# Two channels to a block matrix: the banded convolutions of layers 2 and 3 in four array tiles instead of sixteen

## The chip, the cores and the metric

The kernel runs on one core of one Trainium2 chip. A core has TensorE (PE, matrix products), VectorE (DVE), ScalarE (ACT), GpSimd (POOL), SyncE (SP, which here only issues transfers), and 16 DMA engines that all queues share. The metric is the device time of one launch in microseconds. Everything is fp32.

## The reference

Four layers with residuals act on x of 8 images, 384 channels, 32x32 pixels; each takes a group norm of its input first.

```python
x = x + L0(gn(x))   # 3 depthwise 3x3 convs + 1x1 convs give q, k, v; attention, 8 heads; 1x1; batch norm
x = x + L1(gn(x))   # 4 experts (384 -> 384 -> 384, relu), 2 of them weighted for each pixel
x = x + L2(gn(x))   # depthwise 7x7 convolution, reflected edges, bias
x = x + L3(gn(x))   # below

def L3(x):
    # three branches, k = 1, 3, 5; the channels are split into 4 chunks of 96:
    # chunks 0 and 2 go through a small MLP (96 -> 12 -> 96), chunks 1 and 3 through a depthwise kxk conv
    x1, x2, x3 = branch(x, 1), branch(x, 3), branch(x, 5)
    a = (x1 + x2 + x3).mean((2, 3))
    g = gelu(a @ fusion_w1 + b1) @ fusion_w2 + b2
    w = softmax(g.reshape(8, 384, 3) over the three branches)
    comb = x1 * w[0] + x2 * w[1] + x3 * w[2]
    return einsum("bchw,cd->bdhw", comb, proj_w) + proj_b
```

## The kernel before

Channels lie on partitions, in three tiles of 128 (`ct` 0 to 2); NC is 3, B 8, N 1024 pixels, W and H 32, P 128, HB 4.

Depthwise convolutions are made on TensorE. An image row of 32 pixels lies along partitions (VectorE transposes 32x32 blocks, L985), four channels to a column of 128 partitions. A horizontal convolution of one channel with one row k of its kernel is then a banded 32x32 matrix; the K rows are accumulated in PSUM, each reading the image shifted by one row. TensorE's array is split into 16 tiles of 32x32: partition group i (32 rows of the array) and column group j take the channel that belongs to (i, j, c). So a chunk c of 16 channels is K x 16 matmuls of 256 columns (8 images x 32) or, for unit 1 of layer 3 with half the images a tile, 128 columns. In the trace one fp32 matmul is two instructions: 224 for a chunk with K = 7, 160 for K = 5, 96 for K = 3.

Layer 2 (L1282 on) runs ct over three tiles and c over 8 chunks. Two chunks fill a PSUM group `ps` of four banks, then ScalarE copies it (`evict`, L1236) to `o`; there are two such groups. The weights `w` of a chunk (edges of the reflection folded in by two GpSimd adds, L1052) come by `next_weights` (L1046), three buffers, issued on SP's queue after the chunk that frees one. SP takes its transfers in order, and waits where one of them waits. When all of ct is done, `finish_all` works on its images: `finish` (L1152 on) transposes back on VectorE (L1157), adds bias and residual `r2` (L1159; loaded by SP at L1154 from `r2mem`), takes statistics for the next norm, and stores y to DRAM (L1162). These steps are interleaved with the matmuls of the next ct. During ct 1 `prepare` reads xn of the third channel tile from `x2mem` (L1143) and transposes it for ct 2, in the same VectorE queue.

After the seventh chunk of ct 2 the norm of layer 3 starts for the first two channel tiles (`norm01`): small matmuls (L167), VectorE, GpSimd (L135), then `prepare3` loads y again, ScalarE normalizes it (L200) and VectorE transposes it (L1218). Then comes unit 1 (`convolve3`, L1260), which holds channels of one half tile of the convolved chunks for both halves of the batch, with `finish` of ct 2 and the norm of the third tile beside it, then unit 0, the first whole tile, with the MLPs (L1449) in between, fusion and softmax of the branch weights, and at last the projection (L1653 on, from 3314 us). `reorder` copies y from DRAM to DRAM into the order of the transposed channels, for the 1x1 branch and the residual. `pair(q)` and `begin` fetch and weigh the convolved chunks for the projection.

Channel orders: ORDER_B is the plain order of layer 3's chunks; ORDER_A has partitions and chunks swapped, so that (i, j, c) of a transposed tile comes out in ORDER_B. Layer 1 writes its result `r` in ORDER_A to `r2mem` (`pass_on`, L1000) with the rows permuted, four transfers for each channel tile of an image. The order of instructions on every engine is the program's in these stages.

Of the kernel before, what the change touches and what calls it, by code (L numbers as in the profile page):

```python
# [1 line left out]

# [34 lines left out]

CHUNKS = (1, 3, 0, 2)
ORDER_B = np.concatenate([np.arange(96) + 96 * c for c in CHUNKS])
ORDER_A = ORDER_B.reshape(NC, 4, 4, 8).swapaxes(1, 2).ravel()  # L40
# [32 lines left out]
def conv_mixer_kernel(ctx: ExitStack, tc: tile.TileContext, a: dict, out: bass.AP):  # L73
# [18 lines left out]
    def group_matrix(order, pool, gp, gps):  # L92
# [11 lines left out]
        if order == "A":  # L104
            gta = gp.tile([C // GS, C], FP, name="gta")
            for ct in range(NC):
                cols = slice(ct * P, (ct + 1) * P)
                nc.gpsimd.tensor_copy(
                    gta[:, cols].rearrange("g (i j c) -> g i j c", i=4, j=4),
                    gt[:, cols].rearrange("g (j i c) -> g i j c", i=4, j=4),  # L110
                )
            gt = gta
# [883 lines left out]
    def pass_on(r, b):  # L996

        for ct in range(NC):
            for i in range(4):
                nc.sync.dma_start(  # L1000
                    out=r2mem[ct][:, b, :].rearrange("(j i c) n -> i j c n", i=4, j=4)[i],
                    in_=r[32 * i : 32 * i + 32, ct, :],
                )
# [9 lines left out]
    for b, h in EARLY:  # L1013
# [11 lines left out]

    lw = lwpool.enter_context(
        tc.tile_pool(name="lw", bufs=3, side="right", reuse_waits="tile")
    )
    weights = {}
    ahead = iter(  # L1030
        [(K7, ct, c) for ct in range(NC) for c in range(8)]
        + [(n, unit, c) for unit in (1, 0) for n in KS for c in range(8)]
    )

    def next_weights():
        key = next(ahead, None)
        if key is None:
            return
        w = lw.tile([P, 4, K7, W + len(EDGE)], FP, tag="w", name="w")
        n, unit, c = key  # L1040
        if n < K7:
            w = w.rearrange("p j k w -> p (j k w)")[:, : 4 * n * W].rearrange(
                "p (j k w) -> p j k w", j=4, k=n
            )
        weights[key] = w
        nc.sync.dma_start(out=w, in_=a["w7" if n == K7 else f"w3{n}"][unit, c])  # L1046
        if n < K7:
            return
        rows = w.rearrange("p j k w -> p (j k) w")
        for c0, e0 in ((0, W), (W - R7, W + R7)):  # L1050
            o = rows[:, :, c0 : c0 + R7]
            nc.gpsimd.tensor_tensor(out=o, in0=o, in1=rows[:, :, e0 : e0 + R7], op=ALU.add)  # L1052
# [5 lines left out]
    for b in range(B):  # L1058
        if b == B - 1:
            for _ in range(3):  # L1060
                next_weights()
# [12 lines left out]
    early_pool.close()  # L1074

# [26 lines left out]
    def group(nb):  # L1102

        ps = tp.tile([P, 4, HF], FP, tag="ps", name="ps")
# [18 lines left out]
    def load3():  # L1123
        for name in "k1 k3 k5 bias3 mw1 mb1 mw2 mw2t fw1 fb1 fw2 fb2".split():
# [27 lines left out]
    def finish(ct, b, o, y):  # L1152
        r2 = ty.tile([P, N], FP, tag="r2", name="r2")
        nc.sync.dma_start(out=r2, in_=r2mem[ct][:, b, :])  # L1154
        if y is None:
            y = new_y()
        nc.vector.transpose(img(y), o[:, b])  # L1157
        yield
# [22 lines left out]
    def finish_all(ct, o):  # L1181
# [6 lines left out]
        for b in range(B + lead):  # L1188
            if b < B:
                next(steps[b])  # L1190
            if b >= lead:
                next(steps[b - lead], None)
            if b >= lead - 1:
# [28 lines left out]
    def reorder():  # L1222
        for b in range(B):
            nc.gpsimd.dma_start(
                out=ya0[b].rearrange("(i j c) n -> j i (c n)", i=4, j=4),
                in_=y2mem[b][0].rearrange("(j i c) n -> j i (c n)", i=4, j=4),
            )
            half, q = b // HB, b % HB
            nc.gpsimd.dma_start(
                out=ya1[q].rearrange("(i j c) n -> j i (c n)", i=4, j=4)[2 * half : 2 * half + 2],  # L1230
                in_=y2mem[b][1, 0:64, :].rearrange("(j i c) n -> j i (c n)", i=4, j=2),
            )

    def evict(o, ps, c):
# [4 lines left out]
        )  # L1239

# [3 lines left out]
    def convolve3(unit, n, o):  # L1244
# [6 lines left out]
        for c in range(8):  # L1251
            if c % ncc == 0:
                ps = group(nb)
            w = weights.pop((n, unit, c))
            for k in range(n):
                for j in range(4):
                    for i in range(4):
                        r = slice(32 * i, 32 * i + 32)
                        k0 = 2 - n // 2 + k
                        nc.tensor.matmul(  # L1260
                            ps[32 * j : 32 * j + 32, i, c % ncc],
                            lhsT=w[r, j, k, :], rhs=x[r, 8 * j + c, :, k0 : k0 + H],
                            start=k == 0, stop=k == n - 1,
                        )
            next_weights()
# [13 lines left out]
    with tc.manual_schedule(engines=ORDERED | {mybir.EngineType.Pool}):  # L1279

        for ct in range(NC):
            o = None  # L1282
            for c in range(8):
                if c % 2 == 0:
                    ps = group(B)
                w = weights.pop((K7, ct, c))
                for k in range(K7):
                    for j in range(4):
                        for i in range(4):
                            r = slice(32 * i, 32 * i + 32)  # L1290
                            nc.tensor.matmul(  # L1291
                                ps[32 * j : 32 * j + 32, i, c % 2],
                                lhsT=w[r, j, k, :W], rhs=xts[ct][r, 8 * j + c, :, k : k + H],
                                start=k == 0, stop=k == K7 - 1,
                            )
                next_weights()
# [63 lines left out]
        for j in range(2):  # L1360
# [8 lines left out]
            k1, k3, k5, bias3, mw1, mb1, mw2, mw2t, fw1, fb1, fw2, fb2, projb, proj, projc  # L1369
        ) = for3.values()  # L1370

        def atile(name, shape, parts=P, tag=None):
            return fa.tile([parts, *shape], FP, tag=tag or name, name=name)
# [89 lines left out]
        hidden3(0)  # L1463
        mean, bsum = windows()
# [28 lines left out]
        def branch_weights():  # L1493
# [35 lines left out]
            for i in range(4):  # L1529
                nc.gpsimd.dma_start(  # L1530
                    out=factor[32 * i : 32 * i + 32],
                    in_=fmem.rearrange("(j i c) k n -> i j c k n", i=4, j=4)[i],
# [45 lines left out]
        def begin(unit, q, pool=pre, queue=nc.sync):  # L1578
# [3 lines left out]
            v = pool.tile([P, N], FP, tag=tag, name=tag)  # L1582
# [18 lines left out]
        def weights3(b, pool):  # L1601
# [4 lines left out]
            wm = pre.tile([MR, C], FP, tag="wm", name="wm")  # L1606
# [215 lines left out]
```

## Time and profile before

| what | us |
|---|---|
| median of three runs | 3451.94 (3447.39 to 3453.05) |
| the profiled execution | 3453.2 |
| its span in the trace | 3451.5 |
| layer 2: first to last matmul of L1291 | 2882.4 to 3097.7 |
| its three tiles, ct 0, 1, 2, begin at | 2882.4, 2943.4, 3024.3 |
| unit 1 of layer 3 begins | 3110.9 |
| first MLP matmul; unit 0 begins | 3192.9; 3201.3 |
| projection begins | 3314.1 |

| 2868 to 3452 us, stage | length | PE busy | DVE | ACT | POOL | granted clock |
|---|---|---|---|---|---|---|
| 2868 to 2943 | 75 | 50.1 | 8.8 | 14.8 | 7.1 | 0.84 |
| 2943 to 3024 | 81 | 45.3 | 48.5 | 14.8 | 12.2 | 0.83 |
| 3024 to 3098 | 74 | 48.2 | 37.1 | 15.5 | 11.2 | 0.86 |
| 3098 to 3111 | 13 | 0.1 | 7.4 | 6.5 | 0.0 | 0.59 |
| 3111 to 3193 | 82 | 51.1 | 50.0 | 26.0 | 7.3 | 0.56 |
| 3201 to 3314 | 113 | 85.7 | 27.3 | 50.0 | 20.1 | 0.84 |
| 3314 to 3452 | 138 | 131.7 | 73.0 | 9.7 | 0.0 | 0.98 |

A line of the profile such as "L1291 PE MATMUL ps<-xt,w 32*32 32x256 f32 x5376 | 135.2, 438 | ..." has the program's line, the engine, the operation, what it writes and reads, the array tile and the shape, the number of instructions, their busy time together (overlaps counted once), the mean duration of one in ns, and after the next bar how long the engine had been idle before them and what ended it. "<-issue" is idle time that no wait explains. "SPq" and "PEq" are the sequencers. L numbers are lines of the kernel before.

### The profile page before, as it was taken

The numbers are of one execution on the slowest core, as the hardware profiler recorded it, in microseconds if no ns is written. First come the engines' busy times: TensorE is split into PE (matmuls) and PEld (weight loads), VectorE is DVE, ScalarE is ACT, GpSimd is POOL, SyncE is SP. The second block draws the span as 40 slices with busy tenths as digits, with TensorE's granted clock in tenths as the row PEclk, the third lists the DMA queues.
The fourth block names the chain that finished last, engine by engine and source line by source line (L and its number), as shares of the span: only waits on it lengthen the run. The fifth ranks groups of instructions, "written<-read, shape, count | busy, mean of one in ns | idle before, by whom it ended". The sixth has DMA issues, their size and how long they took to land. (4 is left out here: it accounts for less than half of the span.)

```text
span 3451.5 us, 56137 instructions
## 1 busy us (share of the span) xinstructions
PE 3085.5 (89%) x24960; PEld 1403.8 (41%) x24960; DVE 1610.4 (47%) x2193; ACT 1202.3 (35%) x1147; POOL 140.8 (4%) x320
## 2 busy tenths in 40 slices
PE   3666999999999999999979999999999997555889
PEld 2443334343434343433333444444444444334434
DVE  6778344444454544444442654333333321546164
ACT  3654453535454444445324302122222211123320
POOL 1000000000000000000000000000000000110200
PEclk9998999999999999999989999999999998885989
DMA  6766202011111010110017222022111103556655
GB/s 223 250 235 229 99 21 76 21 60 36 57 39 57 30 61 27 55 42 19 23 49 270 85 90 86 28 67 76 32 63 64 41 8 117 194 171 199 224 198 200
DMA packets 97251, 338.49 MB, mean 98 GB/s; under 512 B 13985, under 2 KB 16777, under 8 KB 92457
## 3 DMA queue, kind: packets, MB, share of 16 engines
q1 hardware_dynamic: 81816, 285.81, 23.9%
q0 software_dynamic: 9184, 32.49, 2.7%
q10 hardware_dynamic: 6000, 16.53, 1.6%
q8 instruction: 197, 3.23, 0.4%
q14 instruction: 54, 0.43, 0.0%
HBM read 236.39 MB, written 101.53 MB: 98 GB/s over the span
## 5 line engine op out<-in xcount | busy, mean ns | idle before, releaser
L548 ACT ACTIVATE e<-sc 128x1024 f32<-128x1024 f32 x512 | 484.2, 1029 | 583.0 <-PE sc L541 582.6
L759 PE MATMUL ph<-xn,w 128*128 128x512 f32 x1152 | 525.0, 594 | 1.2 <-ACT xn L200 1.2
L972 PE MATMUL y<-hs,w 128*128 128x512 f32 x1152 | 519.9, 593 | 1.5 <-DVE hs L957 1.5
L541 PE MATMUL sc<-qT,kT 64*128 64x512 f32 x2048 | 481.7, 607 | 22.1 <-DVE qT L467 15.4
L560 PE MATMUL av<-e,vT 128*64 128x512 f32 x2048 | 468.9, 600 | 0.0
L763 ACT ACTIVATE hs<-ph,b 128x512 f32<-128x512 f32 x192 | 131.7, 686 | 630.9 <-PE ph L759 629.3
L972 PEld LDWEIGHTS y<-hs,w 128*128 128x128 f32 x1152 | 217.8, 190 | 274.4 <-issue 263.5
L759 PEld LDWEIGHTS ph<-xn,w 128*128 128x128 f32 x1152 | 216.3, 190 | 268.3 <-issue 258.8
L541 PEld LDWEIGHTS sc<-qT,kT 64*128 64x128 f32 x2048 | 186.5, 186 | 309.9 <-issue 232.0
L957 DVE TENSOR_TENSOR hs<-hs,cb 128x512 f32<-128x512 f32 x192 | 130.7, 690 | 355.6 <-ACT hs L763 348.6
L560 PEld LDWEIGHTS av<-e,vT 128*64 128x64 f32 x2048 | 135.9, 137 | 318.6 <-issue 318.6
L449 PE MATMUL sc<-y,pw 128*128 128x512 f32 x576 | 254.1, 602 | 12.0 <-DVE kT L467 7.3
L325 PE MATMUL ps<-xt,w 32*32 32x256 f32 x6912 | 161.9, 418 | 106.8 <-issue 106.8
L576 DVE RECIPROCAL inv<-sm 128x512 f32<-128x512 f32 x64 | 214.6, 3353 | 2.2
L1291 PE MATMUL ps<-xt,w 32*32 32x256 f32 x5376 | 135.2, 438 | 82.4 <-POOL w L1052 39.6
L574 DVE LOAD_MASK_SELECT sm<-av x64 | 0.9, 14 | 417.1 <-PE av L560 417.1
L962 DVE SCALAR_TENSOR_TENSOR r<-cb,b,r 128x512 f32<-128x512 f32 x192 | 134.9, 744 | 91.0 <-DMA cb<-cfmem 89.4
L325 PEld LDWEIGHTS ps<-xt,w 32*32 32x32 f32 x6912 | 109.8, 107 | 158.5 <-issue 136.3
L449 PEld LDWEIGHTS sc<-y,pw 128*128 128x128 f32 x576 | 110.4, 193 | 155.2 <-issue 147.2
L350 ACT COPY o<-ps 128x2048 f32<-128x2048 f32 x36 | 134.6, 3739 | 102.0 <-PE ps L325 101.3
L1291 PEld LDWEIGHTS ps<-xt,w 32*32 32x32 f32 x5376 | 91.9, 110 | 124.5 <-issue 56.9
L1236 ACT COPY o<-ps 128x2048 f32<-128x2048 f32 x20 | 73.9, 3694 | 173.2 <-PE ps L1291 151.6
(285 smaller groups left out, 2680.8 us busy)
## 6 DMA issues: line engine op xcount, KB each, us to landing
raw<-y SPq DMA_DIRECT2D x72, 512.0 KB
y<-raw SPq DMA_DIRECT2D x24, 1536.0 KB
xr<-in_x SPq DMA_DIRECT2D x42, 512.0 KB
cb<-cfmem SPq DMA_DIRECT2D x64, 256.0 KB
w<-in_w ACTq DMA_DIRECT2D x36, 384.0 KB
w<-in_w SPq DMA_DIRECT2D x24, 532.0 KB
x<-in_x SPq DMA_DIRECT2D x16, 768.0 KB
z<-z POOLq DMA_DIRECT2D x16, 768.0 KB, 4.3
```

Source lines behind the costliest of these rows:

```text
L325: nc.tensor.matmul(ps[32 * j : 32 * j + 32, i, cc], lhsT=w[r, cc, j, k, :], rhs=xt0s[ct][r, 8 * j + 2 * u + cc, :, k : k + H], start=k == ...
L350: nc.scalar.copy(o.rearrange("p b h (i c) -> p i c (b h)", i=4)[:, :, 2 * u : 2 * u + 2], ps.rearrange("p i c b h -> p i c (b h)"),)
L449: nc.tensor.matmul(ps[:, h, :], lhsT=w[:, ct, pair, :], rhs=y[:, ct, h * HF : (h + 1) * HF], start=ct == 0, stop=ct == NC - 1,)
L541: nc.tensor.matmul(sc[:, s, :], lhsT=kTs[b][r, pair, m * P : (m + 1) * P], rhs=qTs[b][r, pair, h * HF : (h + 1) * HF], start=True, stop=True,)
L548: nc.scalar.activation(e, sc, AF.Exp, scale=1.0 if shifted else HD**-0.5)
L560: nc.tensor.matmul(av[64 * s : 64 * s + 64, :], lhsT=vT[:, m, c0 : c0 + 64], rhs=e[:, s, :], start=m == 0, stop=m == N // P - 1,)
L576: nc.vector.reciprocal(inv, sm)
L759: nc.tensor.matmul(ph, lhsT=w1[:, e, ct, dc * P : (dc + 1) * P], rhs=xn[:, ct, :], start=ct == 0, stop=ct == NC - 1,)
L763: nc.scalar.activation(hs, ph, AF.Relu, bias=b1[:, e, dc : dc + 1])
L962: nc.vector.scalar_tensor_tensor(out=out[oc], in0=cb[e], scalar=b2[:, oc, e : e + 1], in1=out[oc], op0=ALU.mult, op1=ALU.add,)
L972: nc.tensor.matmul(py[oc], lhsT=w2[:, e, dc, oc * P : (oc + 1) * P], rhs=hs, start=k == 0, stop=k == len(TODO) - 1,)
L1291: nc.tensor.matmul(ps[32 * j : 32 * j + 32, i, c % 2], lhsT=w[r, j, k, :W], rhs=xts[ct][r, 8 * j + c, :, k : k + H], start=k == 0, stop=k ...
```

## The change

The convolutions of layers 2 and 3 use a split of the array into four tiles of 64x64. Two channels that lie on neighbouring groups of 32 partitions form a block diagonal matrix of 64x64, with zeros off the diagonal. The loop over (j, i), 16 matmuls for each k, becomes e in 0, 1 and (d, i) in 2 x 2, 8 matmuls for each k, each writing 64 partitions. In instructions: 112 a chunk instead of 224 in layer 2 (2688 instead of 5376), 80 and 48 instead of 160 and 96 in layer 3 (2048 instead of 4096 in all).

The block matrices are made on the chip: the bands are loaded as before (`load_weights`, two buffers, now issued from ScalarE's queue save the first two), GpSimd folds the edges in, and ScalarE copies every loaded part twice with a 0/1 scale by partition (`parity`), once into the left 32 columns and once into the right ones. A part is half a chunk for K = 7 and 5, and a whole one for K = 3; three buffers `wx`. The channel order ORDER_A follows the new layout (halves of 64 instead of quarters of 32), and layer 0's tables get the old one as ORDER_0. Transfers that permute rows change their shapes: those to `r2mem` (2x16x1024 instead of 4x8x1024 elements), `reorder` (24 instead of 16) and the fusion factors. `finish` is split so that r2 is loaded after the transpose, two images ahead. To make room, fw1 and fw2 are loaded later into an x1 buffer, `q` and `win` move into an output buffer, and `pair(1)` moves from the convolution of unit 0 into the projection. The tables for the group norms are permuted with six GpSimd copies instead of three.

```diff
-ORDER_A = ORDER_B.reshape(NC, 4, 4, 8).swapaxes(1, 2).ravel()
+ORDER_A = ORDER_B.reshape(NC, 2, 2, 2, 16).swapaxes(1, 3).ravel()
+ORDER_0 = ORDER_A.reshape(NC, 4, 4, 8).swapaxes(1, 2).ravel()
...
                 nc.sync.dma_start(
-                    out=r2mem[ct][:, b, :].rearrange("(j i c) n -> i j c n", i=4, j=4)[i],
+                    out=r2mem[ct][:, b, :].rearrange("(d b a r) n -> a b d r n", a=2, b=2, d=2)[
+                        i // 2, i % 2
+                    ],
                     in_=r[32 * i : 32 * i + 32, ct, :],
                 )
...
-        tc.tile_pool(name="lw", bufs=3, side="right", reuse_waits="tile")
+        tc.tile_pool(name="lw", bufs=2, side="right", reuse_waits="tile")
     )
+    parity = lw.tile([P, 2], FP, name="parity", bufs=1)
+    nc.gpsimd.memset(parity, 0.0)
+    for i in range(4):
+        nc.gpsimd.memset(parity[32 * i : 32 * i + 32, i % 2 : i % 2 + 1], 1.0)
+    WPARTS = {K7: 2, 5: 2, 3: 1}
+    weights, loaded = {}, []
+    todo_load = [(K7, ct, c) for ct in range(NC) for c in range(8)]
+    todo_load += [(n, unit, c) for unit in (1, 0) for n in KS for c in range(8)]
+
+    def load_weights(queue=nc.scalar):
+        if not todo_load:
+            return
+        k, unit, c = todo_load.pop(0)
+        rows, cols = 4 * k, W + (len(EDGE) if k == K7 else 0)
+        w = lw.tile([P, 4 * K7, W + len(EDGE)], FP, tag="w", name="w")
+        w = w.rearrange("p r w -> p (r w)")[:, : rows * cols].rearrange("p (r w) -> p r w", w=cols)
+        queue.dma_start(out=w, in_=a["w7" if k == K7 else f"w3{k}"][unit, c])
+        if k == K7:
+            for c0, e0 in ((0, W), (W - R7, W + R7)):
+                o = w[:, :, c0 : c0 + R7]
+                nc.gpsimd.tensor_tensor(out=o, in0=o, in1=w[:, :, e0 : e0 + R7], op=ALU.add)
+        n = rows // WPARTS[k]
+        for e in range(WPARTS[k]):
+            loaded.append(((k, unit, c, e), w[:, n * e : n * e + n, :W]))
 
     def next_weights():
-        key = next(ahead, None)
-        if key is None:
+        if not loaded:
             return
...
-        nc.sync.dma_start(out=w, in_=a["w7" if n == K7 else f"w3{n}"][unit, c])
...
+        key, w = loaded.pop(0)
+        n = w.shape[1]
+        x = wx.tile([P, 2 * K7, 2, W], FP, tag="wx", name="wx")
+        for t in range(2):
+            nc.scalar.activation(x[:, :n, t, :], w, AF.Copy, scale=parity[:, t : t + 1])
+        weights[key] = x.rearrange("p r t w -> p r (t w)")
+        if key[3] == WPARTS[key[0]] - 1:
+            load_weights()
...
     def finish(ct, b, o, y):
-        r2 = ty.tile([P, N], FP, tag="r2", name="r2")
-        nc.sync.dma_start(out=r2, in_=r2mem[ct][:, b, :])
         if y is None:
             y = new_y()
         nc.vector.transpose(img(y), o[:, b])
+        yield
+        r2 = ty.tile([P, N], FP, tag="r2", name="r2")
+        nc.sync.dma_start(out=r2, in_=r2mem[ct][:, b, :])
         yield
...
+            for i in range(2):
+                nc.gpsimd.dma_start(
+                    out=ya0[b].rearrange("(d b a r) n -> b a d (r n)", a=2, b=2, d=2)[i],
+                    in_=y2mem[b][0].rearrange("(a b d r) n -> b a d (r n)", a=2, b=2, d=2)[i],
+                )
...
-                w = weights.pop((K7, ct, c))
-                for k in range(K7):
-                    for j in range(4):
-                        for i in range(4):
-                            r = slice(32 * i, 32 * i + 32)
+                for e in range(2):
+                    w = weights.pop((K7, ct, c, e))
+                    for k in range(K7):
+                        for d, i in product(range(2), repeat=2):
+                            r = slice(64 * i, 64 * i + 64)
                             nc.tensor.matmul(
-                                ps[32 * j : 32 * j + 32, i, c % 2],
-                                lhsT=w[r, j, k, :W], rhs=xts[ct][r, 8 * j + c, :, k : k + H],
+                                ps[64 * d : 64 * d + 64, 2 * i + e, c % 2],
+                                lhsT=w[r, d * K7 + k, :],
+                                rhs=xts[ct][r, 16 * d + 8 * e + c, :, k : k + H],
                                 start=k == 0, stop=k == K7 - 1,
                             )
-                next_weights()
+                    next_weights()
...
         hidden3(0)
+
+        fws = new_x1().rearrange("p c b h -> p (c b h)")
...
+        nc.gpsimd.dma_start(out=fw1, in_=a["fw1"])
+        nc.gpsimd.dma_start(out=fw2, in_=a["fw2"])
...
-                None, None, lambda: pair(0, pre, nc.gpsimd), output_bias,
-                lambda: pair(1, pre, nc.gpsimd), None, first,
+                None, None, lambda: pair(0, pre, 1, nc.gpsimd), output_bias, None, None, first,
...
-            if q + 2 < HB and half == 0:
-                pair(q + 2, py)
+            if q + 1 < HB and half == 0:
+                pair(q + 1, py, HB - 1)
```

## What was predicted before the run

> **What bounds the kernel now.** I read the page first (busy shares, slices, costliest groups), then a table of engine time by stage, then waits and timelines of the stages that the change touches. All but the last 583 us are attention and experts, which the change leaves to TensorE as they are. It works on 2882 to 3314 us, the three channel tiles of layer 2 (ct0, ct1, ct2), then unit 1 and unit 0 of layer 3's convolutions. From the page:
>
> ```profile
> PE   3666999999999999999979999999999997555889
> PEclk9998999999999999999989999999999998885989
> ...
> L541 PE MATMUL sc<-qT,kT 64*128 64x512 f32 x2048 | 481.7, 607 | 22.1 <-DVE qT L467 15.4
> L560 PE MATMUL av<-e,vT 128*64 128x512 f32 x2048 | 468.9, 600 | 0.0
> ...
> L1291 PE MATMUL ps<-xt,w 32*32 32x256 f32 x5376 | 135.2, 438 | 82.4 <-POOL w L1052 39.6 <-issue 37.6 <-POOL xt L988 5.1
> ```
>
> The first rows say that PE is only half busy here (555 against 9) and its clock is not always granted. The L1291 line is the one of the group view cut to layer 2: 135.2 us of matmuls, 82.4 of idle. Nearly half of the idle ends at a weight tile, the rest is PE's own issuing. A PE timeline shows that part: 128 matmuls in 2.8 us, then a gap.
>
> ```profile
> 2949.18 2.86 PE L1291 MATMUL ps<-xt,w 32*32 32x256 f32 x128 [0.67 <-issue]
> 2952.76 2.79 PE L1291 MATMUL ps<-xt,w 32*32 32x256 f32 x128 [0.73 <-issue]
> 2956.78 2.82 PE L1291 MATMUL ps<-xt,w 32*32 32x256 f32 x127 [1.23 <-issue]
> ```
>
> So 128 take some 3.6 to 3.9 us, 29 ns each, and a channel chunk of 224 some 6.5 to 7.3. The other half of the story is VectorE, here by stage and then in its own timeline:
>
> ```profile
> 2943.00:3005.00 62.00, 34.55 (x1378) 22.86 (x1354) 48.52 (x64) 14.82 (x4) 6.29 (x20) 0.86 0.64 215
> 3005.00:3028.00 23.00, 13.75 (x567) 9.96 (x570) 0.00 (x0) 3.30 (x1) 5.94 (x26) 0.78 0.42 147
> 3028.00:3065.00 37.00, 20.34 (x827) 12.97 (x817) 34.12 (x56) 7.88 (x3) 3.02 (x12) 0.88 0.64 207
> ```
>
> ```profile
> 2947.60 4.62 DVE L1157 STREAM_TRANSPOSE x<-o 128x1024 f32<-128x1024 f32 x4 [63.88 <-ACT o L1236]
> ...
> 3004.28 0.36 DVE L1174 TENSOR_REDUCE edges<-y 128x4 f32<-128x128 f32 x1
> 3028.50 4.62 DVE L1157 STREAM_TRANSPOSE x<-o 128x1024 f32<-128x1024 f32 x4 [23.87 <-issue]
> ```
>
> (Columns of the first: window, length, then busy time of PE, weight loads, DVE, ACT, POOL, clock, DMA share, GB/s.) DVE works through ct0's outputs from 2947.6 to 3004.6, 57 us of which 8 wait for xn loads; then it has nothing for 23.9 us because PE is late with ct1; then 36.5 us for ct1's outputs. PE and DVE take turns at being late, and PE's part is what can shrink.
>
> **What the Trainium skill says.** "TensorEngine Tiling (Array Packing)", Tiling Modes, lists 64x64 as four independent tiles. The trace has no such tile, but its two-tile modes agree: L541 and L560 are two at a time, 481.7/2048 and 468.9/2048, about 232 ns for one of a pair, and the chain of waits has a plain 128x512 at 429 ns. A 256-column one should thus take 215 ns, and four at once 54 ns each. "TensorE: Matmul & The Clock Gate", Part 1, says that the array drops to half clock after idling and needs some 3.4 us of work to come back; the clock column (0.86, 0.78, 0.56 in unit 1) agrees that thin work runs slower. "DMA: Bandwidth & Descriptors", "Why a DMA increments its semaphore by 16 and not by 1", says that a queue transfer uses the largest number of engines up to 16 that divides the slowest dimension on both sides. The r2mem writes agree: 4x8x1024 moves at about 105 GB/s, four engines of 4 KB per 159 ns. As 2x16x1024 they would have two.
>
> **The change, part by part.**
>
> 1. Matmuls of layer 2: 2688 instead of 5376. A chunk is 112 x 54 = 6.05 us at full clock against about 7.1; eight are 48.4. Stream-bound now, not issue-bound: at half clock the chunk would be 12. The weight gaps: loads were in SP's queue behind r, y and xn transfers that wait for DVE. Now they follow ACT's copies, free of these: I take the 39.6 us as mostly gone.
> 2. Making the block matrix: two ACTIVATEs of 448 elements for each half chunk. ACT's 1024-element one with one pointer is 1144 ns (L1586), 512 elements 678 (L1457), so 0.6 each, 2.4 us a chunk; half an eviction 1.85, one load issue 0.33. 4.6 of 6.05 us: it fits, but not by much. Behind an ACTIVATE that waits for its loaded tile stand the evictions and xn; evictions hold both PSUM groups. Two chunks ahead cover some 9 us of load time. I take +6 us over both layers for weights that come late (0 to +25).
> 3. Start: the first matrices stand behind xn on ACT, +2 us; the first 3.4 us at half clock cost 3.
> 4. r2mem writes (L1000): 12 writes of 131 KB an image at four engines take 15 us; at two, 30. The SP timeline and DVE's of one image:
>
> ```profile
> 2231.16 11.18 SPq L1000 DMA_DIRECT2D r<-r  x12
> 2249.19 0.32 SPq L938 DMA_DIRECT2D cb<-cfmem  x1
> 2249.73 1.27 SPq L738 DMA_DIRECT2D r<-z  x3
> ...
> 2259.96 2.48 DVE L741 SCALAR_TENSOR_TENSOR r<-r,zn_s,xr 128x1024 f32<-128x1024 f32 x2
> ```
>
> With two engines the backlog ends at about 2264. cb is used at 2267.7, so it is in time; r is used at 2260 and comes 4 to 5 us late. Behind L741 on DVE stands hs, whose slack is one pass of y and ph, 5.15 less ACT and DVE, 3.5 us. So 1 us in each of five images, +5 (0 to +25). At the start of layer 2 the third chunk's weights, issued at about 2885, wait for the same backlog until 2899: +4.
> 5. ct0 then ends at 2884.4 + 48.4 + 3 + 4 = 2940 instead of 2943.8. DVE starts after the 3.7 us eviction and needs its 57 us: 3001. xt of ct2 is complete at 44.4 us of these, so PE starts ct2 at about 2989, right after ct1 (2988). DVE goes on with ct1's outputs without the 23.9 us hole: 3001 + 36.5 = 3037 instead of 3065. PE ends ct2 at 3038 to 3040. So the norm's matmuls start at 3040 instead of 3082.1. From there to unit 1 the chain is the old one, 28 us (statistics, POOL, two y loads, xn, transposes; the end of it here):
>
> ```profile
> 3097.35 2.37 ACT L200 ACTIVATE xn<-xn,pair_t,pair_s 128x1024 f32<-128x1024 f32 x2 [11.36 <-DVE pair_t L1318]
> ...
> 3110.92 3.27 PE L1260 MATMUL ps<-x,w 32*32 32x128 f32 x152 [13.23 <-DVE x L1218]
> ```
>
> Unit 1 starts at 3068 instead of 3110.9: -43, the bulk of the forecast. Bounds -30 (DVE waits more for xn) and -52 (a shorter norm chain).
> 6. Unit 1: 1024 instead of 2048 matmuls of 128 columns. At half clock, which it has now, 54 ns each, 55 us, against 71 of 3111 to 3188 without the norm. DVE's finishing of ct2 (45 us) and norm3 lie on its path too, so I take half: -8 (0 to -14).
> 7. Unit 0: 1024 x 54 = 55 us against 52 busy and 9 of issue gaps: -6 (+5 to -10; the 7.3 us stall behind an eviction stays).
> 8. Reordering by GpSimd: 24 transfers for 16, twice the bytes a row; 26 us long before, waited for much later: 0. finish() loads r two images ahead and after the transpose: part of 5. fw1 and fw2 move to a later GpSimd load, whose user comes some 55 us after: 0. pair(1) moves into the projection: +1 to +2 of DVE and ACT there, against PE which is busy 131.7 of 138: +1. Layer 0's other order: same instructions but three GpSimd copies: 0.
>
> Sum: -43 - 8 - 6 + 6 + 5 + 1 = -45. The profiled execution took 3453.2 (span 3451.5), 1.3 above the median shown: 3453.2 - 45 - 1.3 = 3407.
>
> **Rivals.** (a) The forecast, 3390 to 3422: DVE takes over from PE as the bound of layer 2. Chance 0.5.
> (b) Weights and xn still come late: transfers share the engines (0.64 busy in DVE's stages), and ACT's queue passes each delay on to evictions. Then the 39.6 us of weight waits mostly come back at other places, and what remains is the shorter issue, 24 x 1 us, plus 14 in layer 3, less 11 of parts 2 and 4: 3425, up to 3448. For it: ACT is 4.6 of 6.05. Against: SP's waits for DVE are out of the weights' way. 0.22.
> (c) Everything behind PE: layer 2 in 145 + 10 us instead of 215, with DVE's xn waits (8 us) gone and a shorter norm: -75, 3377. Against: DVE's 57 + 36.5 us are there. 0.14.
> (d) Slower: four tiles do not run at once, or run at half clock, 107 ns each. Place: layer 2 and unit 0. Layer 2 is then 24 x 12 = 288 us instead of 215, +73, and unit 0 110 instead of 61, +49: 3574. It decides from some 75 ns on: 2688 x 75 is 202, 13 below the old 215, and 1024 x 75 is 77, 16 above the old 61. At 90 ns it is +27 and +31: 3510. For it: the clock is below full throughout this stage, and now the rate hangs on it; loading 64 columns takes 137 ns (L560), so loads must overlap. Against: in attention both pairs fill the array at a clock of 0.99 and 1.00, and the present tiles keep 12 and more in flight. 0.09.
> (e) Part 4 is not hidden: 15 us in each of 8 images, +120 for the +5 above, net 3522; at some two fifths of it no gain is left. 0.05.
>
> **Chances.** A measurement of this kernel tells about 0.2% (7 us) from nothing. Faster: (a), (c) and most of (b), 0.82; same 0.04, from (b)'s end; slower 0.14, (d) and (e). The range of 8 in 10 cuts half of (c) and (d) and (e) away: 3376 to 3446.
>
> **What would show it.** In the trace after: L1291's 2688 matmuls at 54 ns a piece (145 us busy together), chunks of 6 to 6.5 us; no wait of over 4 us for weights; DVE's 23.9 us hole gone; first norm matmul at about 3040, unit 1 at 3068, projection at about 3262. The forecast is wrong if PE waits for the block matrices (ACT becomes the releaser of L1291), if the clock stays at half, if r2mem's slow writes hold up layer 1 (layer 2 starting after 2900), or if DVE's 57 us grow by waits for xn.

## The result and the profile after

| | before | changed |
|---|---|---|
| median, 20 runs each (us) | 3451.23 | 3456.82 |
| profiled execution, span | 3451.5 | 3450.7 |

The ratio of changed to before is 1.0019, interval 1.0012 to 1.0026: 0.2% slower where 1.3% faster was forecast, and outside the range of 3376 to 3446. The spans of the two profiled executions lie the other way round by 0.8 us, within the scatter of single executions, so stages are compared below, not totals.

First the groups of layer 1 and layer 2 on TensorE, from the changed kernel's page. Its line numbers are higher by 4 in layer 1 (L957, L962 and L972 are now L961, L966 and L976), and L1291 is now L1327.

```profile
L976 PE MATMUL y<-hs,w 128*128 128x512 f32 x1152 | 530.9, 603 | 25.9 <-DVE hs L961 25.9
...
L1327 PE MATMUL ps<-xt,wx 64*64 64x256 f32 x2688 | 162.2, 401 | 41.6 <-ACT wx L1068 41.4
```

The tiles do what was expected of them: 2688 matmuls, none of the old idle time by issue, 41.6 us of idle instead of 82.4. But layer 1, whose matmuls are the old ones, has 25.9 us of waits for `hs`; before it was 1.5. The timeline of PE into layer 2, changed kernel, with the idle time before each stretch in brackets:

```profile
2910.61 8.50 PE L1327 MATMUL ps<-xt,wx 64*64 64x256 f32 x112 [7.20 <-ACT wx L1068]
2930.65 82.82 PE L1327 MATMUL ps<-xt,wx 64*64 64x256 f32 x1456 [11.54 <-ACT wx L1068]
3029.63 39.75 PE L1327 MATMUL ps<-xt,wx 64*64 64x256 f32 x672 [16.16 <-ACT wx L1068]
```

Layer 2 begins at 2910.6 instead of 2882.4, PE then waits 11.5 us for its second chunk (a chunk is 112 instructions) and later 16.2 us, ahead of the seventh chunk of ct 1. In the long stretch 1456 matmuls take 82.8 us, 57 ns each. Whatever the tiles gain is set against a late start. How the stages stand, from the traces' start times (layer 1 from first to last y matmul, the others from first matmul to first matmul; MLP is the first matmul of the MLPs, L1449 and now L1493; one profiled execution for each kernel):

| us | layer 1 | layer 2 to unit 1 | unit 1 to MLP | MLP to projection | projection to end |
|---|---|---|---|---|---|
| before | 916.5 | 228.5 | 82.0 | 121.2 | 137.4 |
| changed | 952.9 | 212.8 | 68.8 | 120.8 | 137.7 |

The 36.4 us lost in layer 1 take back all of what layer 2 (15.7) and unit 1 (13.2) gave, and 7.5 more; ahead of layer 1 the changed kernel was 10.2 us earlier in this execution, which is taken up below. What layer 1 waits for is seen in one image. SyncE's queue of the changed kernel, where the prediction showed that of the kernel before (start, length of the issuing, transfers):

```profile
2227.95 17.34 SPq L1004 DMA_DIRECT2D r<-r  x12
...
2246.30 3.62 SPq L942 DMA_DIRECT2D cb<-cfmem  x1
2261.31 1.27 SPq L742 DMA_DIRECT2D r<-z  x3
```

and VectorE's timeline of the same image, changed kernel:

```profile
2254.07 0.69 DVE L961 TENSOR_TENSOR hs<-hs,cb 128x512 f32<-128x512 f32 x1 [4.46 <-ACT hs L767]
2263.07 2.08 DVE L966 SCALAR_TENSOR_TENSOR r<-cb,b,r 128x512 f32<-128x512 f32 x3 [8.30 <-DMA cb<-cfmem]
2265.06 2.48 DVE L745 SCALAR_TENSOR_TENSOR r<-r,zn_s,xr 128x1024 f32<-128x1024 f32 x2
```

The same place in the kernel before, where nothing is waited for:

```profile
2257.97 2.07 DVE L962 SCALAR_TENSOR_TENSOR r<-cb,b,r 128x512 f32<-128x512 f32 x3
```

The transfers of `r` to `r2mem` take 17.3 us to issue instead of 11.2, cb is issued at 2246.3, and VectorE stands 8.3 us until it lands at 2263. And from tables by window, with DMA share and GB/s as the last two columns, of the changed kernel and of the kernel before while only these writes move:

```profile
2230.00:2245.00 15.00, 14.56 (x56) 7.99 (x55) 9.81 (x19) 5.49 (x6) 1.37 (x3) 1.00 0.13 50
```

```profile
2233.00:2246.00 13.00, 12.48 (x50) 7.04 (x50) 7.80 (x19) 3.75 (x4) 0.85 (x1) 1.00 0.26 100
```

0.13 of 16 engines at 50 GB/s is two engines, 0.26 at 100 GB/s is four. That is what the rule that the prediction took from the Trainium skill, "DMA: Bandwidth & Descriptors", section "Why a DMA increments its semaphore by 16 and not by 1", gives for 2x16 and 4x8 rows: the largest number up to 16 that divides the slowest dimension on both sides.

### The profile page after: what moved, and what is told of

Read it like the earlier page. It is cut to its first block, busy times and chain, and to the rows that moved or that the text cites. A ratio compares the mean times of both kernels' runs of the same rounds, so it can differ in the third digit from the quotient of the medians.

```text
span 3450.7 us, 46880 instructions
## 1 busy us (share of the span) xinstructions
PE 3128.2 (91%) x20224; PEld 1427.4 (41%) x20224; DVE 1609.7 (47%) x2193; ACT 1304.5 (38%) x1339; POOL 151.4 (4%) x337
## 5 line engine op out<-in xcount | busy, mean ns | idle before, releaser
L976 PE MATMUL y<-hs,w 128*128 128x512 f32 x1152 | 530.9, 603 | 25.9 <-DVE hs L961 25.9
L976 PEld LDWEIGHTS y<-hs,w 128*128 128x128 f32 x1152 | 220.3, 193 | 307.0 <-issue 263.6
L961 DVE TENSOR_TENSOR hs<-hs,cb 128x512 f32<-128x512 f32 x192 | 130.5, 689 | 344.8 <-ACT hs L767 338.5
L453 PE MATMUL sc<-y,pw 128*128 128x512 f32 x576 | 253.8, 602 | 11.3 <-DVE kT L471 6.6
L329 PE MATMUL ps<-xt,w 32*32 32x256 f32 x6912 | 166.2, 431 | 96.8 <-issue 96.8
L1327 PE MATMUL ps<-xt,wx 64*64 64x256 f32 x2688 | 162.2, 401 | 41.6 <-ACT wx L1068 41.4
L966 DVE SCALAR_TENSOR_TENSOR r<-cb,b,r 128x512 f32<-128x512 f32 x192 | 134.9, 745 | 136.2 <-DMA cb<-cfmem 134.7
L329 PEld LDWEIGHTS ps<-xt,w 32*32 32x32 f32 x6912 | 113.7, 109 | 149.0 <-issue 125.4
L354 ACT COPY o<-ps 128x2048 f32<-128x2048 f32 x36 | 134.4, 3735 | 95.5 <-PE ps L329 92.3
L1068 ACT ACTIVATE wx<-w,parity 128x448 f32<-128x448 f32 (+2 forms) x192 | 108.1, 615 | 125.9 <-DMA r<-r 29.9
L1327 PEld LDWEIGHTS ps<-xt,wx 64*64 64x64 f32 x2688 | 106.2, 141 | 96.5 <-ACT wx L1068 37.0
```

Source lines behind the costliest of these rows:

```text
L329: nc.tensor.matmul(ps[32 * j : 32 * j + 32, i, cc], lhsT=w[r, cc, j, k, :], rhs=xt0s[ct][r, 8 * j + 2 * u + cc, :, k : k + H], start=k == ...
L354: nc.scalar.copy(o.rearrange("p b h (i c) -> p i c (b h)", i=4)[:, :, 2 * u : 2 * u + 2], ps.rearrange("p i c b h -> p i c (b h)"),)
L453: nc.tensor.matmul(ps[:, h, :], lhsT=w[:, ct, pair, :], rhs=y[:, ct, h * HF : (h + 1) * HF], start=ct == 0, stop=ct == NC - 1,)
L966: nc.vector.scalar_tensor_tensor(out=out[oc], in0=cb[e], scalar=b2[:, oc, e : e + 1], in1=out[oc], op0=ALU.mult, op1=ALU.add,)
L976: nc.tensor.matmul(py[oc], lhsT=w2[:, e, dc, oc * P : (oc + 1) * P], rhs=hs, start=k == 0, stop=k == len(TODO) - 1,)
L1327: nc.tensor.matmul(ps[64 * d : 64 * d + 64, 2 * i + e, c % 2], lhsT=w[r, d * K7 + k, :], rhs=xts[ct][r, 16 * d + 8 * e + c, :, k : k + H], ...
```

## The experiments

"Whole rows" below is the kernel of the first experiment, on which most others build. The ratio is always to the kernel before, measured on the same chip in the same set of runs.

**1. The r2mem writes in whole rows of 16.** In the changed kernel:

```diff
-            for i in range(4):
+            for i, d in product(range(4), range(2)):
                 nc.sync.dma_start(
                     out=r2mem[ct][:, b, :].rearrange("(d b a r) n -> a b d r n", a=2, b=2, d=2)[
-                        i // 2, i % 2
+                        i // 2, i % 2, d
                     ],
-                    in_=r[32 * i : 32 * i + 32, ct, :],
+                    in_=r[32 * i + 16 * d : 32 * i + 16 * d + 16, ct, :],
```

> The changed kernel with its r2mem writes cut in two, so that each writes 16 whole rows instead of 2x16. Theory A (the two-engine writes cost layer 1 its 28 us and the start of layer 2 another 8 to 11): the writes spread over 16 engines, TensorE's waits for hs in layer 1 fall from 25.9 us to under 3, layer 2 starts within 3 us of 2882, the wait for the fourth block matrix goes, and the time is 3410 to 3422, ratio to before 0.988 to 0.992. Rival B (the writes are not the cause, or twice as many issues on SP cost the same): layer 2 still starts after 2900 and the time is 3445 or more.

Measured: 3401.91 us against 3450.35, ratio 0.986 (0.9843 to 0.9876). Layer 1 is 913.9 us, PE waits 0.2 us for hs in it, and layer 2 starts at 2875.3. While these writes move, from 2225 to 2234 us, 0.73 of the 16 engines are busy, at 127 GB/s. PE's timeline into layer 2:

```profile
2875.32 88.38 PE L1327 MATMUL ps<-xt,wx 64*64 64x256 f32 x1568 [7.49 <-ACT wx L1068]
2981.82 11.17 PE L1327 MATMUL ps<-xt,wx 64*64 64x256 f32 x168 [18.12 <-ACT wx L1068]
```

1568 matmuls, fourteen chunks of 112, run without a stop, where the changed kernel stopped after one chunk for 11.5 us; the later stop of 16 to 18 us remains. Theory A holds, and its gain was larger than expected, with the time below its range and layer 2 starting 7 us before 2882: 51 us between the two spans, 39 in layer 1 and 14.6 in ct 0 (65.8 to 51.2 us), less 3 elsewhere.

**2. The kernel before with nothing but the new form of these writes.** In the kernel before the destination of L1001 is replaced by the changed kernel's `"(d b a r) n -> a b d r n"` with `[i // 2, i % 2]`.

> The kernel before with only the r2mem writes in the changed kernel's form, 12 writes of 2x16x1024 an image (so layer 2 adds rows of r that belong to other channels; the rest is as before). Theory A: two engines at some 52 GB/s, cb comes 5 us late in each image, layer 2 starts 25 to 30 us later and loses another 0 to 8 us at its start behind the backlog: 3478 to 3490, ratio 1.008 to 1.011. Rival B (the loss in layer 1 comes from something else in the change): within 3 us of before.

Measured: 3493.67 us, ratio 1.0122 (1.0098 to 1.0146), a little above A's range. Layer 1 is 951.6 us, 35.1 more, and layer 2 to unit 1 takes 233.4, 4.9 more, 3.1 of it in ct 0 (64.2 for 61.1). PE's waits in layer 1 of this run:

```profile
PE y L972 <- DVE hs L957: 24.3, 8, 4.9
```

It is the same wait, of nearly the same length, as in the changed kernel, made by one line and without any block matrix. With experiment 1 this settles the loss in layer 1: the shape of one transfer. The 14.6 us in ct 0 also go with the shape, as experiment 1 shows, but the kernel before loses only 3.1 there; the rest needs something of the changed kernel besides, which the account of the prediction below names.

**3 and 4. Weight loads from GpSimd's queue, without and with whole rows.** The later stop asks for its own test. It lies after fourteen chunks, so ahead of the seventh chunk of ct 1, the middle tile; the expectations below put it in the last tile. In the trace ScalarE does not wait for data there. ScalarE's and SyncE's queues with whole rows:

```profile
2958.41 1.23 ACT L1068 ACTIVATE wx<-w,parity 128x448 f32<-128x448 f32 x2
2980.08 0.34 ACTq L1052 DMA_DIRECT2D w<-in_w  x1
2980.53 2.35 ACT L1068 ACTIVATE wx<-w,parity 128x448 f32<-128x448 f32 x4 [20.90 <-DMA r<-r]
```

```profile
2975.36 0.32 SPq L1188 DMA_DIRECT2D y<-y  x1
2975.73 0.42 SPq L1183 DMA_DIRECT2D r<-r  x1
```

ScalarE has nothing else to do from 2959.6 until it issues the load at 2980.08. The load goes when an r load of SyncE's queue has landed, which SyncE could issue only at 2975.7, after a y that VectorE had to finish. Neither its buffer nor its data have to do with that r. The two share a completion semaphore: the trace's records give number 109 to the r of 2975.73 and to the load of 2980.08, and ScalarE waits for 109 just before it. The edit:

```diff
-    def load_weights(queue=nc.scalar):
+    def load_weights(queue=nc.gpsimd):
```

> The changed kernel with the weight loads issued from GpSimd's queue instead of ScalarE's, nothing else. Theory C (ScalarE's issue waits for a completion slot whose last user is a transfer in SP's queue that itself waits for VectorE, so the wait of 21.1 us at 3007 is one of order and not of bandwidth): the waits of L1327 for wx over 4 us in the last tile of layer 2 go, 16 + 5 us less there, and part of it reaches the end: 10 to 20 us faster than the changed kernel, 3437 to 3447. Layer 1 stays as slow as in the changed kernel. Rival D (the loads are late because the DMA engines are full): the same stall shows with GpSimd in place of ScalarE, and the time is 3453 to 3460 or above.

> Both edits, whole-row writes of r2mem and weight loads from GpSimd's queue. Theories A and C together: the gains add, 3395 to 3410, ratio 0.983 to 0.988. If D holds it equals the kernel with whole-row writes alone; if B holds it equals the kernel with GpSimd's loads alone.

Measured: 3487.18 us, ratio 1.0103 (1.0086 to 1.012), and 3447.85 us, ratio 0.9991 (0.9982 to 1.0): both 30 to 46 us worse than with ScalarE's queue, and both expectations missed. By stages the theory on order is right and its end wrong. With whole rows, layer 2 to unit 1 goes from 196.2 to 189.8 us and no wait for wx in layer 2 is over 7.5. But from the first MLP matmul to the projection it takes 168.0 us instead of 120.0. GpSimd's timeline there:

```profile
3155.92 0.55 POOL L1052 DMA_DIRECT2D w<-in_w  x1 [17.90 <-ACT wx L1068]
3156.47 2.08 POOL L1485 DMA_DIRECT2D y<-y  x4
```

A weight load waits in GpSimd's queue for a free buffer, and the four y transfers behind it, which the MLP needs, wait with it (PE waits 20.2 us for them in five places, and 17.2 us once for a block matrix; in experiment 1 it has neither wait there). A load that waits for its buffer holds up what is behind it, and in this queue that was urgent.

**5 and 6. Only layer 2's loads from GpSimd's queue, and only its last ten.** On whole rows, first the edit of 5, then that of 6, ahead of the issue in `load_weights`:

```diff
+        if k == K7 and queue is nc.scalar:
+            queue = nc.gpsimd
```

```diff
+        if k == K7 and (unit, c) >= (1, 6):
+            queue = nc.gpsimd
```

> Whole-row writes of r2mem, and the weight loads of layer 2 alone (7x7) from GpSimd's queue; those of layer 3 stay on ScalarE's. Theory: GpSimd's queue helped layer 2 (no wait of 18 us for wx; layer 2 to unit 1 in 190 us instead of 196) and hurt only layer 3, where the reorder transfers stood behind weight loads in it. Then layer 2 takes 189 to 192 us, layer 3 as with ScalarE's loads, and the time is 3392 to 3399. Rival: the loss in the run with all loads from GpSimd comes from software-issued loads as such (slower landing), and shows in layer 3 of this run too or eats layer 2's gain: 3402 or more.

> Whole-row writes of r2mem, and only the loads for the last ten chunks of layer 2 from GpSimd's queue (the one that ScalarE waited 20.9 us to issue is the second of them). If that wait is one of order only, TensorE's 18.1 us stall in the last tile goes and the short waits that all of GpSimd's loads brought in the middle tile stay away: layer 2 to unit 1 in 180 to 188 us, 3384 to 3394. If VectorE's 57 us of the middle tile set the end of layer 2 anyway, the stall only moves: 190 to 196 us, 3394 to 3402.

Measured: 3402.83 us, ratio 0.9859 (0.9836 to 0.9883), and 3405.13 us, ratio 0.9859 (0.9837 to 0.9882): no difference from whole rows alone. The first time is the one that the rival expected, though whether for its reason is not shown; the second missed both ranges. Layer 2 to unit 1 is 192.7 and 198.0 us. PE's waits there, first with whole rows alone, then with layer 2's loads on GpSimd:

```profile
PE ps L1327 <- ACT wx L1068: 31.9, 5, 18.1
```

```profile
PE ps L1329 <- ACT wx L1070: 18.9, 9, 7.5
PE ps L171 <- DVE mv L1193: 7.4, 1, 7.4
```

The stop of 18 us is gone, a wait for VectorE's last statistics of 7.4 us has come, and unit 1 starts only 3 us closer to the start of layer 2 in one run and 2 us further in the other. So the order in the queues made the stop, but the stop wasn't what layer 2 cost.

**7. The kernel before with whole rows of its own**, 24 writes of 16 rows:

> The kernel before with its r2mem writes in whole rows of 16, 24 instead of 12. If four engines already hid these writes before, layer 1 is 0 to 3 us shorter and the time within 4 us of before, 3446 to 3453. If they cost something there too, it is 8 us or more faster. The convolutions of layer 0, the same instructions in all kernels here, end at 313.6 in the kernel before and at 307.6 to 309 in the changed ones: if the cause is in the kernels, they end after 312 here; if it is scatter, they may end anywhere between.

Measured: 3448.32 us, ratio 0.9994 (0.998 to 1.0008), layer 1 914.4 us. This is what was expected if four engines already hid these writes, and two do not. Layer 0's last convolution starts at 311.9 us here, just outside "after 312". Over all profiled executions it starts between 311.9 and 316.8 in the three with the kernel before or its variants, and between 303.9 and 312.9 in the eleven with the changed one or its variants; layer 1 starts between 1951.2 and 1955.7 in the three and between 1942.5 and 1950.5 in the eleven, 6.6 us earlier in the mean. These ranges do not overlap, so of the 10 us that the changed kernel was ahead before layer 1, a good part seems to go with the kernel. The forecast had put this at nothing ("Layer 0's other order: same instructions but three GpSimd copies: 0"), and what causes it was not found.

**8. Statistics over 64 of 1024 pixels**, to take VectorE out of layer 2's end:

```diff
-        bn_stats_of(bs, y)
+        for h in range(2):
+            nc.vector.bn_stats(bs[:, h, :], y[:, 32 * h : 32 * h + 32])
```

> The kernel with whole-row writes of r2mem and the weight loads on ScalarE's queue, in which the statistics of layer 2's outputs are taken over 64 of the 1024 pixels only (this part of the norm of layer 3 is left out): 1.2 us less of VectorE for each image and channel tile, 9.6 in the middle tile, 9.6 in the last, 9.6 beside unit 1. If VectorE's chain with its loads sets the end of layer 2 (theory a), layer 2 to unit 1 takes 176 to 188 us instead of 196 and the time is 3380 to 3394. If TensorE and ScalarE's block matrices set it, layer 2 stays within 4 us and only unit 1 gains: 3394 to 3402.

Measured: 3402.69 us, ratio 0.9861 (0.984 to 0.9882), layer 2 to unit 1 196.8 us: no gain, as the second theory has it, with the time 0.7 above its range. In layer 2 VectorE's waits for r and xn grow from 11.3 us with whole rows to 21.4, so some 10 of the 19 us that it was to save there come back as waits for loads; the rest is idle time at other places. Less of VectorE's own work did not make layer 2 shorter.

**9. The 2x16 form of the changed kernel, issued from GpSimd's queue**, `nc.sync` replaced by `nc.gpsimd` in the r2mem writes:

> The changed kernel with its r2mem writes in their 2x16 form, but issued from GpSimd's software queue. If the loss in layer 1 comes from SP's transfers (cb, r, xr) standing behind a backlog on the same two engines, then with the writes on whatever engines GpSimd's queue picks[...], layer 1 is within 6 us of the kernel with whole rows and the time 3400 to 3415. If it is the form itself wherever it is issued, or GpSimd's rsqrt comes late behind its issues, layer 1 keeps 15 us or more of the loss: 3420 or above.

Measured: 3408.91 us, ratio 0.9885 (0.9857 to 0.9914), layer 1 916.3 us, and 1.7 us of waits for hs, all as the first theory has it. The window of the writes in this run, columns as above:

```profile
2230.00:2242.50 12.50, 11.98 (x49) 6.85 (x48) 6.87 (x18) 1.37 (x2) 7.04 (x12) 1.00 0.53 122
```

Of the two queues tried the form is slow on SyncE's only: from GpSimd's the same writes keep 0.53 of the engines busy, at 122 GB/s. The intervals of this run and of whole rows overlap.

**10. Layer 2's loads on GpSimd (5) and short statistics (8) together.**

> Both edits that did nothing alone: layer 2's weight loads on GpSimd's queue and statistics over 64 of 1024 pixels (that part of the norm of layer 3 is left out), with whole-row writes of r2mem. If two chains end layer 2 almost together (TensorE behind its block matrices, VectorE behind its loads and statistics), removing a part of both shows: layer 2 to unit 1 in 176 to 187 us against 193 to 198 in the three kernels before, and 3380 to 3395. If one thing that neither touches sets the end (the loads of r and xn through SP's queue, or TensorE's own 153 us with the norm's chain behind), it stays at 190 or more and the time at 3396 to 3404.

Measured: 3402.15 us, ratio 0.9861 (0.984 to 0.9882), layer 2 to unit 1 190.8 us. Time and stage are those of the second theory. The wait for the last statistics falls from 7.4 to 4.5 us, more was not there: two nearly equal chains aren't the whole answer.

**11 and 12. Half of each 7x7 weight tile loaded**, on 10 and on whole rows alone; both halves of a chunk use the same bands:

```diff
-        rows, cols = 4 * k, W + (len(EDGE) if k == K7 else 0)
+        rows, cols = (2 if k == K7 else 4) * k, W + (len(EDGE) if k == K7 else 0)
...
-        n = rows // WPARTS[k]
+        n = 4 * k // WPARTS[k]
         for e in range(WPARTS[k]):
-            loaded.append(((k, unit, c, e), w[:, n * e : n * e + n, :W]))
+            r0 = 0 if k == K7 else n * e
+            loaded.append(((k, unit, c, e), w[:, r0 : r0 + n, :W]))
```

> The kernel of the run before (whole rows, layer 2's weights from GpSimd's queue, short statistics), which in addition loads half of each 7x7 weight tile and uses it for both halves of the chunk (layer 2 computes with wrong bands for every second channel pair): 6.5 MB less to move in layer 2, GpSimd's edge adds half as long. If the landing of weights (4 to 8 us a load at 242 to 248 GB/s) holds the rest of layer 2, layer 2 to unit 1 takes 172 to 184 us instead of 190.8, time 3380 to 3395. If not, it stays within 4 us: the floor is then TensorE's 153 us, the end of layer 1's chain and the norm's 28 us.

> Whole-row writes of r2mem, all weight loads on ScalarE's queue and full statistics, with only the halved 7x7 weight loads of the other run. If moved bytes set the end of layer 2, it gains here too, 8 us or more of 196; if ScalarE's wait for SP's order (18 us) and VectorE's chain do, it stays within 4 us, at 3396 to 3405.

Measured: 3400.9 us, ratio 0.9839 (0.982 to 0.9858), and 3407.52 us, ratio 0.986 (0.9836 to 0.9885). The kernel before took 3460.26 us on this chip, so the ratios are to be compared, and both overlap that of whole rows. Layer 2 to unit 1 is 183.2 us with all three, within the range of the first theory, which missed the time, and 190.1 with the halved loads alone, between the two ranges. PE's waits in layer 2 of experiment 11:

```profile
PE ps L1331 <- ACT wx L1071: 14.4, 7, 7.2
PE ps L1298 <- DVE x L1253: 12.4, 1, 12.4
PE ps L171 <- DVE mv L1195: 4.3, 1, 4.3
```

Taken one at a time against 196.2, loads on another queue give 3.4 us, short statistics -0.6, half the weights 6.1; all three give 13.0, in the stage, and no more than a few us in total. Each figure is from one execution, and experiments 5 and 6, which do nearly the same, differ by 5.3 us, so the single ones are not clear of scatter. None of the three alone explains what layer 2 takes. Of these 183 us, PE's matmuls are some 153 (2688 at 57 ns), 7.2 are waits for wx (the other 7.2 lie ahead of the first matmul), and 16.7 the two waits around the norm. That one more thing lies behind these three isn't excluded.

## Why the prediction was wrong, point by point

**The step that failed is the r2mem one** (part 4). Its mechanism in layer 1 was right: two engines, a backlog of some 30 us, transfers of the same queue behind it. Its size was wrong: it was priced at +5 in layer 1 and +4 at layer 2's start, and measured +36.4 (35.1 in experiment 2, where it is alone) and +14.6, some 51 together. Three things were missed.

First, a misreading in one sentence: "cb is used at 2267.7, so it is in time". In the kernel before:

```profile
2263.23 0.33 SPq L938 DMA_DIRECT2D cb<-cfmem  x1
...
2267.70 1.42 DVE L962 SCALAR_TENSOR_TENSOR r<-cb,b,r 128x512 f32<-128x512 f32 x2 [0.27 <-DMA cb<-cfmem]
```

The wait at 2267.7 is that of the cb issued at 2263.2. The one before it, issued at 2249.2, was used at 2258.0 by L962, in the line shown with the result, which waits for nothing and so names no releaser. A transfer with 9 us of slack was taken for one with 18. Counted from the first of the writes, VectorE is ready for that cb after 26.8 us in both kernels; the prediction's backlog ends after 33, and in the changed kernel cb has landed after 35.1. So VectorE is 7.6 to 8.3 us late in each of six images. Behind it hs has the 3.5 us of slack that the prediction gave it, and little more: TensorE waits 3.9 to 4.6 us at this place in five images. All its waits for hs are 25.9 us, against 1.5 before.

Second, what such a wait costs afterwards. The first y matmuls after one of them, and six others soon after, in the changed kernel:

```profile
2268.20 5.38 PE L976 MATMUL y<-hs,w 128*128 128x512 f32 x6 [4.59 <-DVE hs L961]
...
2275.99 2.74 PE L976 MATMUL y<-hs,w 128*128 128x512 f32 x6
```

The granted clock is 1.00 from 2240 to 2260 us, 0.67 from 2268 to 2276 and 1.00 again from 2276 to 2290, and it falls in the same way at all five waits; in the kernel before it is 1.00 from 2000 to 2860. The y matmuls are busy 530.9 us instead of 519.9, 11 us that come on top of the waits. In each of the five images the next one begins 133.4 to 135.0 us later instead of 127.2 to 127.8, and the last image is 2.4 us longer. The prediction named the slower clock after idling and charged it at layer 2's start, not here.

Third, at layer 2's start the loss took another path than the one priced. The prediction has the third chunk's weights wait for the backlog. TensorE stops ahead of the second chunk already, for 11.5 of the 14.6 us, because ScalarE, which makes its block matrix, stands still:

```profile
2917.76 5.29 SPq L219 DMA_DIRECT2D k<-in_k  x3
```

```profile
2929.55 0.33 ACTq L1052 DMA_DIRECT2D w<-in_w  x1
2929.93 1.79 ACT L1068 ACTIVATE wx<-w,parity 128x448 f32<-128x448 f32 x3 [17.74 <-DMA k<-in_k]
```

ScalarE waits 17.7 us before it may issue its next load, until a small load of SyncE's queue, issued behind the r2mem writes, has landed. The two have only a completion semaphore in common (number 103), as the load and the r of experiments 3 and 4 have. With whole rows this wait is 1.2 us. The prediction took ScalarE's loads to be free of what SyncE's queue waits for (part 1); at these two places they were not.

The rival (e) had named the loss at +120 with a chance of 0.05 and said that some two fifths of it would leave no gain; 51 of 120 it was.

**The other terms came near in sum, in part by luck.** Without this term the forecast was 54 us less than before; experiment 1 measured 48 less, 3401.91 to 3450.35, and its span is 51.7 less. But 7.9 of the 51.7 lie ahead of layer 1, where the forecast has nothing (experiment 7), and 2.6 in layer 1; layer 2, the bulk of the forecast, gave 12 to 16 us less than it should. In its parts, from experiment 1 where no other kernel is named:

- Matmuls of 54 ns each (part 1): 56 in the stretch of 1568, with a granted clock of 1.00 from 2890 to 2963 us; 57 in that of the changed kernel. Rival (d), tiles that do not run together or stay at half clock, is refuted.
- ScalarE's block matrices (part 2): 96 ACTIVATEs of 448 elements are busy 58.5 us, 0.61 each; 0.6 were taken. In the stretch of fourteen chunks they fit. The wait behind a load was foreseen in words, but for a late landing, not for a transfer of another queue.
- Layer 2 to unit 1 (part 5): 228.5 became 196.2, where the text has 2884 to 3068, 184, or 180 without the backlog's 4. Tile by tile ct 0 took 51.2 us for 51.4, ct 1 70.0 for 49, and from ct 2 to unit 1 it was 74.9 for 79. The miss is ct 1: it has the stop of 18.1 us (without which, in experiments 5 and 6, other waits came), and VectorE's hole of 23.9 us shrank to 14.0 and did not vanish. That VectorE takes over as the bound (a) is not shown, and late weights (b) are not the whole of it either: experiments 5 to 12 find several limits within a few microseconds of each other.
- Unit 1 (part 6): 82.0 to 71.2 us, 10.7 less against 8.
- Unit 0 (part 7): 1.2 less against 6, from the first MLP matmul to the projection. 160 matmuls of 256 columns are 9.0 us, 56 ns each; the 320 of before took 10.6 in one such place, gaps included. Part of such a gain of 1.6 us turns into a new wait for an eviction, twice 0.9 us.
- The projection (part 8): 137.4 to 137.1 us, +1 was taken.

## What to carry to other kernels

When a change alters the shape of a transfer, work out how many engines the new shape uses, and then find for every transfer behind it in the same queue the instruction that first reads it, also where that instruction waits for nothing: slack is measured to the reader, not to the next wait that the profile shows. Add to a wait of TensorE's what the clock costs after it: here 11 us on 24. A transfer of rows can be cut into pieces of 16 rows, which here was worth 1.6% of the kernel (0.986 against 1.0019). And a load that waits for its buffer belongs in a queue where nothing urgent stands behind it: in GpSimd's queue it cost 46 us (experiment 4).

## What the traces showed that was not expected

A load on ScalarE's queue waited 20.9 us for a transfer that SyncE had not yet issued when the wait began (experiment 1's trace), and the same loads on GpSimd's queue did not (no wait for r in ScalarE's list in experiment 5). The records of these traces say why: from layer 2 on, the transfers of SyncE's and of ScalarE's queue take the same eight completion semaphores in turn, those of GpSimd's queue eight others. In both places shown above the load waits for the semaphore that it takes, until its last user has landed. So the two queues are coupled in order, though not in their data, by the waits that the program holds.

The same 2x16 transfers moved 50 GB/s from SyncE's queue and 122 from GpSimd's.

In layer 1 of the changed kernel a wait of some 4 us on TensorE cost 6 to 7 us, and at each the granted clock fell (to 0.52 from 2669 to 2676 us, for one).
